# Regrouping the gelu pass of a two-layer spectral-attention block on Trainium2: both mixes, both first transforms, both groups of transposes, then the next synthesis

## The chip, the core and the metric

One core of a Trainium2 chip runs the whole kernel in one launch. The metric is the device time of an execution in microseconds. The kernel before was timed in five runs; its median is 575.03 us (572.42 to 576.11). Its profile is of one execution of 575.71 us, whose instructions span 573.7 us.

## The reference

The input x is (2, 56, 128, 128) in float32: two images with 56 planes of 128 x 128. Two layers of the same form follow each other. In each, all operators work by the plane, with a spectral convolution that keeps 32 x 16 modes. Cut to what matters here:

```
def layer(x):
    xn = inorm(x)                                   # per plane
    k, q, v = fno(xn, K), fno(xn, Q), fno(xn, V)     # 8 heads
    out = softmax(q k^T / 128) v                    # over the 56 planes
    att = inorm(fno(out, P) + x)
    an = inorm(att)
    h = gelu(inorm(spectral(an, M0)) + skip(an))    # over 128 x 128
    h = inorm(spectral(h, M1)) + skip(h)
    return inorm(h) + att

x = x + layer(group_norm(x))    # twice, with two sets of weights
```

The gelu stage is the line of h with gelu: it needs a plane's values in space, applies gelu to them, and the next line needs the modes of the result.

## The kernel before, in words

All arithmetic is float32. Each of the two images (b = 0 and 1) has a working plane tile P[b] of 128 x 8192, and X2 holds the input of both. Work on modes is done by TensorE (PE) with small matrices. Spatial values are formed by two sets of matmuls that add up in PSUM: `synthesis` (matmul at L751) turns modes into space, and `mixed` (L766) adds the attention's mix of the 56 planes of X2.

A gelu pass handles one image in four steps A = 0 to 3, each with two halves v = 0 and 1 of 128 x 1024 values. For each A:

- `synthesis(A)`: 16 matmuls into two PSUM pairs, one for each half (32 records in the trace, because each float32 matmul appears as two).
- `mixed(A, v)`: 4 matmuls onto a pair; then ScalarE (ACT) applies gelu from the pair into P[b] (L819), and VectorE (DVE) takes statistics of it, two instructions per half (L821).
- `turn_back(A, v)`: 8 transposes on PE (L801) of the gelu's result into another pair, and a copy on ACT into one of the two buffers hT[v] (L802).
- `forward(A, v)`: 4 matmuls (L789) from hT[v], the first transform of the next convolution, into a bank shared by both halves; after the second half a DVE copy to FB[b] (L794).

A pair is two PSUM banks. The pool of pairs has three buffers, the pool of single banks has two[...]. A new pair therefore waits until the pair three allocations ago has been read.

The order of the work is written out by hand in generators. Each `yield` gives a planned cost; `_woven` takes a leading chain (small dependent steps) and runs units of the bulk generators between its steps until the cost that the chain asks for is used up. In each layer there are two gelu passes: gelu(0), woven with `norms_chain` of image 1 (sums at L441, scalar steps on DVE and a square root on ACT at L721, spread of rows at L436, DVE steps L729 to L743, inverse at L401 with stream transposes on DVE at L406); and gelu(1), woven with `h_chain` of image 0 (L835 to L876, modes at L386, product at L419, sums at L441, square roots at L859 and L866, spread at L436, a scale at L878 copied at L880, inverse at L401). The inverse of each chain makes the modes from which the next pass's synthesis starts. After the second pass follows `end`, in which synthesis and mix are done once more, DVE (L916) and GpSimd (L918) add the terms, and the DMA queue of SyncE moves the result out (L896).

A scheduler puts the instructions on each engine's queue, largely in the order in which they are issued, but it lets an instruction pass others where its own inputs are ready earlier.[...]

Of the kernel before, what the change touches and what calls it, by code (L numbers as in the profile page):

```python
# [166 lines left out]
def fno_layers(ctx: ExitStack, tc: tile.TileContext, x, out, weights, small, const):  # L167
# [13 lines left out]
    def bank():  # L181
        return ps.tile([N, 512], F32, name="bank")

    def pair():
        return pq.tile([N, 2, 512], F32, name="pair")
# [267 lines left out]
    def new_stats(b):  # L453
        return little(f"stats{b}", [N, 16, 6])
# [292 lines left out]
    def synthesis(A, both, Z):  # L747
        for e in range(4):
            for j in range(4):
                o = 64 * (8 * A + 2 * e)  # L750
                T.matmul(  # L751
                    both[j // 2][:, j % 2, N * e : N * e + N], lhsT=Z[32 * j : 32 * j + 32, o : o + N],
                    rhs=C["gw"][32 * j : 32 * j + 32, :], start=(e == 0), stop=False, tile_position=(32 * j, 0),
                    skip_group_check=True,
                )

    def mixed(L, b, A, v, p, Bs):

        for c in range(2):
            s = 16 * A + (8 * v + 4 * c if L == 0 else 8 * c + 4 * v)
            for r in range(2):
                q = slice(64 * r, 64 * r + K + 1)
                T.matmul(  # L766
                    p[64 * c : 64 * c + 64, r, :], lhsT=Bs[q, :], rhs=X2[q, b, s : s + 4, :].rearrange("p e w -> p (e w)"),
                    start=False, stop=True, tile_position=(64 * r, 64 * c), skip_group_check=True,
                )

    def gelu(L, b, st):
        stats = st["stats"] = new_stats(b)
        banks = {}

        def at(A, v):
            return P[b][:, 2048 * A + 1024 * v : 2048 * A + 1024 * v + 1024]

        def forward(A, v):
            if v == 0:
                banks[A] = bank()  # L780
            f1, t = banks[A], hT[v]
            for q in range(4):
                if L == 0:
                    dst = f1[32 * q : 32 * q + 32, 224 * v : 224 * v + 224].rearrange("p (r m) -> p r m", r=2)
                    src = t[:, :, q].rearrange("p r c k -> p r (c k)")
                else:
                    dst = f1[32 * q : 32 * q + 32, :448].rearrange("p (c j k) -> p c j k", c=2, j=4)[:, :, 2 * v : 2 * v + 2]
                    src = t[:, :, q].rearrange("p r c k -> p c r k")
                T.matmul(  # L789
                    dst, lhsT=C["fw"], rhs=src, start=(v == 0), stop=True, tile_position=(0, 32 * q),  # L790
                    skip_group_check=True,
                )
            if v == 1:
                V.tensor_copy(FB[b][:, 448 * A : 448 * A + 448], f1[:, :448])  # L794

        def turn_back(A, v):
            h3, p = at(A, v), pair()
            for r in range(2):
                for e in range(4):
                    o = 512 * r + N * e  # L800
                    T.transpose(p[:, r, N * e : N * e + 120], h3[:120, o : o + N], ident[:120, :120])  # L801
            S.copy(  # L802
                hT[v].rearrange("p r e c k -> p (r e) c k"),
                p.rearrange("p r (e c k) -> p (r e) c k", e=4, c=2)[:, :, :, :K],
            )

        for A in range(6):
            if A < 4:
                both = [pair(), pair()]
                synthesis(A, both, st["Z"])  # L810
                yield 1.0
            if A > 1:
                forward(A - 2, 1)
                yield 0.4
            for v in range(2):
                if A < 4:
                    mixed(L, b, A, v, both[v], st["Bs"])
                    h3 = at(A, v)
                    S.activation(h3, both[v].rearrange("p r m -> p (r m)"), AF.Gelu)  # L819
                    for r in range(2):  # L820
                        V.bn_stats(stats[:, 4 * A + 2 * v + r, :], h3[:, 512 * r : 512 * r + 512])  # L821
                    yield 0.9
                if 0 < A < 5:
                    turn_back(A - 1, v)
                    yield 0.8
            if 0 < A < 5:
                forward(A - 1, 0)
                yield 0.4

    def h_chain(L, b, st):  # L830
        (par, d), fb, D = prs[L], FB[b], st["D"]
# [102 lines left out]
    st = [[{}, {}], [{}, {}]]  # L934
# [8 lines left out]
    for L in range(2):  # L943
        s0, s1 = st[L]
        more = relay(cpt, tcs, stage[:, :1024], [(16, 16), (32, 4)]) if L == 0 else ()
        _run(_woven(chain(modes_chain(L, 1, stats[1], s1), more), gram(0, s0)))
        build(WTv, tcs, 16, range(0, 8, 2))
        build_m(tcs)
        _run(_woven(gram_chain(L, 0, s0), _with(gram(1, s1), scale_x(0, s0))))
        _run(_woven(gram_chain(L, 1, s1), scores(L, 0, s0)))  # L950
        _run(_woven(softmax_chain(L, 0, s0), values(L, 0, s0)))
        _run(_woven(mix_chain(L, 0, s0), heads(L, 0, s0)))
        _run(_woven(
            norms_chain(L, 0, s0), _with(scores(L, 1, s1), scale_x(1, s1)),
            _woven(softmax_chain(L, 1, s1), values(L, 1, s1)), _woven(mix_chain(L, 1, s1), heads(L, 1, s1)),
        ))
        if L == 0:
            nc.sync.dma_start(out=stage[:, :1088], in_=weights[1].rearrange("p m r n t -> p (m r n t)"))
            par, d, cpt, tcs = prepare(1, G, G)
            prs[1] = par, d  # L960
        _run(_woven(norms_chain(L, 1, s1), gelu(L, 0, s0)))
        _run(_woven(h_chain(L, 0, s0), gelu(L, 1, s1)))
        stats = [new_stats(b) for b in range(B)] if L == 0 else [None, None]
        more = relay(cpt, tcs, stage[:, :1024], [(0, 16), (16, 16), (32, 4)]) if L == 0 else ()
        _run(_woven(chain(h_chain(L, 1, s1), more), end(L, 0, s0, stats[0])))
        if L == 0:
            o = _PARTS["fx"][0]
            nc.sync.dma_start(out=Ct[:, o:], in_=const["all"][:, N_CONST:])
            build(WUv, tcs, 0, range(0, 8, 2))
            _run(_woven(modes_chain(1, 0, stats[0], st[1][0]), end(0, 1, s1, stats[1])))  # L970
        else:
            _run(end(1, 1, s1, None))
# [52 lines left out]
```

## Time and profile before

| What | Value |
|---|---|
| median of five runs | 575.03 us |
| lowest and highest | 572.42, 576.11 us |
| the profiled execution, its own time | 575.71 us |
| its span, first to last instruction | 573.7 us |
| mean granted clock of TensorE | 0.88 of full speed |
| busy share of PE, DVE, ACT, POOL | 82%, 58%, 33%, 32% |
| gelu(0), layer 0 (first synthesis to the next pass's) | 173.0 to 206.1 us |
| gelu(1), layer 0 | 206.1 to 243.0 us |
| gelu(0), layer 1 | 440.4 to 471.4 us |
| gelu(1), layer 1 | 471.4 to 508.2 us |

A busy PE is a time in which matmul records lie open. It says nothing on the clock at which they run; that is a column of its own, PEclk, in tenths or as a share of full speed. In a timeline, a line is a run of like instructions: start, duration, engine, line of the code, operation, output and inputs, shapes, number of records, and in brackets the idle time ahead of it with what ended it. PEld are the weight loads of PE, which run beside the matmuls.

### The profile page before, as it was taken

How to read it: one execution, taken by the hardware profiler on the slowest of the kernel's cores; microseconds unless marked ns; L12 is line 12 of the kernel's file. 1: busy time of each engine (PE TensorE's matmuls, PEld its weight loads, DVE VectorE, ACT ScalarE, POOL GpSimd, SP SyncE). 2: the span in 40 equal slices, each digit the busy share in tenths (PEclk: the TensorE clock that was granted, in tenths of full speed). 3: DMA queues.
4: the chain of work that ended last, by engine and by line, in shares of the span. 5: the costliest groups of instructions: out<-in, count | busy, mean ns of one | idle time of the engine just before them, and what ended most of it. 6: DMA issues, size and time to landing. Idle time of an engine off the chain costs nothing.

```text
span 573.7 us, 15727 instructions
## 1 busy us (share of the span) xinstructions
PE 468.7 (82%) x7110; PEld 322.3 (56%) x7110; DVE 333.9 (58%) x577; ACT 191.2 (33%) x238; POOL 181.3 (32%) x190
## 2 busy tenths in 40 slices
PE   2446989889989999888587949987999999979480
PEld 1422949649866555545473447755957555645240
DVE  0576478811335774778649995831161767584661
ACT  2334131150536456413203314114343755712000
POOL 2450516800083000054375761620000000016566
PEclk9999689785997998998768969978799999898596
DMA  8992000050000000036334631040000000006687
GB/s 207 207 205 31 4 1 3 3 141 3 3 3 2 2 1 1 1 81 210 113 98 127 193 110 27 3 103 2 2 2 3 1 2 1 2 18 192 193 247 283
DMA packets 16307, 40.64 MB, mean 71 GB/s; under 512 B 2528, under 2 KB 3296, under 8 KB 16224
## 3 DMA queue, kind: packets, MB, share of 16 engines
q1 hardware_dynamic: 15520, 38.25, 24.7%
q10 hardware_dynamic: 720, 1.39, 1.0%
q8 instruction: 56, 0.92, 0.7%
q14 instruction: 11, 0.09, 0.1%
HBM read 24.69 MB, written 14.68 MB: 69 GB/s over the span
## 4 chain that ended last, share of the span: by engine, by line
PE 46%; DVE 20%; DMA 11%; ACT 6%; issue 6%; POOL 6%; SPq 3%; POOLq 1%; ACTq 0%; DVEq 0%
PE pair L766 6%; PE pair L801 5%; PE pair L595 5%; DVE X L550 4%; PE pair L689 4%; PE pair L751 4%; PE bank L511 3%; PE bank L576 3%; DVE stats L373 3%; POOL X L918 3%; SPq L896 3%; PE bank L789 3%; DMA xr<-x 3%; POOL P L918 2%; DMA X<-store 2%
## 5 line engine op out<-in xcount | busy, mean ns | idle before, releaser
L821 DVE BATCH_NORM_STATS2 stats<-P 128x6 f32<-128x512 f32 x64 | 40.5, 680 | 21.5 <-ACT P L819 21.4
L916 DVE SCALAR_TENSOR_TENSOR P<-P,hs,pair 128x1024 f32<-128x1024 f32 x32 | 40.1, 1269 | 18.1 <-PE pair L766 18.1
L550 DVE TENSOR_TENSOR X<-X,gvr 120x1024 f32<-120x1024 f32 x32 | 48.7, 1550 | 0.0
L918 POOL TENSOR_TENSOR X<-P,xr 128x1024 f32<-128x1024 f32 x16 | 39.1, 2450 | 29.5 <-DVE P L916 14.3
L373 DVE BATCH_NORM_STATS2 stats<-P 128x6 f32<-128x448 f32 x64 | 35.7, 612 | 19.8 <-ACT P L368 10.1
L819 ACT ACTIVATE P<-pair 128x1024 f32<-128x1024 f32 x32 | 32.6, 1026 | 33.6 <-PE pair L766 33.0
L801 PEld LDWEIGHTS pair<-C,P 120*128 120x128 f32 x256 | 28.3, 149 | 23.3 <-issue 12.3
L395 POOL MEMSET WT<- 128x256 f32 x4 | 1.3, 313 | 124.7 <-PE bank L789 89.9
L766 PE MATMUL pair<-X,Bs 57*64 57x512 f32 x256 | 40.1, 668 | 0.0
L511 PE MATMUL bank<-P 128*64 128x56 f32 (+1 forms) x1024 | 38.8, 244 | 0.0
L511 PEld LDWEIGHTS bank<-P 128*64 128x64 f32 (+1 forms) x1024 | 37.2, 158 | 2.9 <-issue 2.6
L766 PE MATMUL pair<-X,Be 57*64 57x512 f32 x256 | 38.1, 692 | 0.0
L595 PEld LDWEIGHTS pair<-xf,WU 64*64 64x64 f32 x1024 | 34.6, 142 | 5.1 <-issue 4.2
L595 PE MATMUL pair<-xf,WU 64*64 64x56 f32 x1024 | 37.3, 227 | 0.0
L801 PE MATMUL pair<-C,P 120*128 120x120 f32 x256 | 36.3, 287 | 0.4 <-ACT P L819 0.2
L751 PE MATMUL pair<-C,WT 32*128 32x128 f32 x512 | 26.3, 312 | 12.4 <-DVE P L916 7.4
L751 PEld LDWEIGHTS pair<-C,WT 32*128 32x128 f32 x512 | 21.2, 207 | 24.5 <-DVE P L916 10.6
L802 ACT COPY WT<-pair 128x896 f32<-128x896 f32 x32 | 28.8, 906 | 13.6 <-PE pair L801 13.3
L363 PE MATMUL pair<-C,X 56*128 56x56 f32 x256 | 17.4, 292 | 18.9 <-DMA X<-x 12.9
L341 POOL TENSOR_TENSOR WT<-tc,C 128x1024 f32<-128x1024 f32 x8 | 26.5, 3341 | 20.0 <-ACT tc L335 11.9
L371 ACT COPY P<-pair 128x896 f32<-128x896 f32 x16 | 14.4, 902 | 47.1 <-PE pair L365 47.1
L363 PEld LDWEIGHTS pair<-C,X 56*128 56x128 f32 x256 | 14.9, 198 | 24.4 <-DMA X<-x 12.3
(249 smaller groups left out, 884.2 us busy)
## 6 DMA issues: line engine op xcount, KB each, us to landing
X<-x SPq DMA_DIRECT2D x16, 448.0 KB
xr<-x SPq DMA_DIRECT2D x32, 224.0 KB
store<-X SPq DMA_DIRECT2D x32, 224.0 KB
out<-P SPq DMA_DIRECT2D x32, 224.0 KB
xr<-store SPq DMA_DIRECT2D x16, 224.0 KB
X<-store SPq DMA_DIRECT2D x16, 224.0 KB
C<-const_all ACTq DMA_DIRECT2D x1, 621.0 KB
stage<-weights ACTq DMA_DIRECT2D x1, 544.0 KB
```

The lines of the kernel that those rows point to most:

```text
L363: T.transpose(p[:, c, o : o + K], X2[q, b, i, :], ident[q, q], tile_position=(64 * c, 0))
L373: V.bn_stats(stats[:, 2 * g + s, :], dst[:, 448 * s : 448 * s + 448])
L511: T.matmul(p[u : u + m, :K], lhsT=P[b][:, K * i : K * i + m], rhs=plane[b][:, i, :], start=(i < 2), stop=(i == N - 1), tile_position=(0, u ...
L550: V.tensor_tensor(v, v, _bc(st["gvr"][:120], 1, 8), ALU.mult)
L595: T.matmul(p[64 * e : 64 * e + 64, k, K * a : K * a + K], lhsT=WUv[64 * e : 64 * e + 64, t + k, a, :], rhs=xv[64 * e : 64 * e + 64, t + k, ...
L751: T.matmul(both[j // 2][:, j % 2, N * e : N * e + N], lhsT=Z[32 * j : 32 * j + 32, o : o + N], rhs=C["gw"][32 * j : 32 * j + 32, :], start ...
L766: T.matmul(p[64 * c : 64 * c + 64, r, :], lhsT=Bs[q, :], rhs=X2[q, b, s : s + 4, :].rearrange("p e w -> p (e w)"), start=False, stop=True, ...
L801: T.transpose(p[:, r, N * e : N * e + 120], h3[:120, o : o + N], ident[:120, :120])
L819: S.activation(h3, both[v].rearrange("p r m -> p (r m)"), AF.Gelu)
L821: V.bn_stats(stats[:, 4 * A + 2 * v + r, :], h3[:, 512 * r : 512 * r + 512])
L916: V.scalar_tensor_tensor(h3, h3, st["hs"], both[v].rearrange("p r m -> p (r m)"), ALU.mult, ALU.add)
L918: G.tensor_tensor(dst, h3, back(n), ALU.add)
```

## The change

The four kinds of work of a pass are kept, and their number too. In the kernel before, the halves of different steps alternate: one mix, one group of transposes, the second mix, the second group of transposes, and the two first transforms at the end of this round and after the next synthesis. In the changed kernel a round does both mixes of A, then both first transforms of A-2, then both groups of transposes of A-1, then the synthesis of A+1. The first synthesis stands ahead of the loop. The planned costs are joined accordingly (1.8 for two mixes, 0.9 for two first transforms, 1.7 for two groups of transposes, 1.0 for a synthesis).

```diff
+        both = [pair(), pair()]
+        synthesis(0, both, st["Z"])
+        yield 1.0
         for A in range(6):
             if A < 4:
-                both = [pair(), pair()]
-                synthesis(A, both, st["Z"])
-                yield 1.0
-            if A > 1:
-                forward(A - 2, 1)
-                yield 0.4
-            for v in range(2):
-                if A < 4:
+                for v in range(2):
                     mixed(L, b, A, v, both[v], st["Bs"])
                     h3 = at(A, v)
                     S.activation(h3, both[v].rearrange("p r m -> p (r m)"), AF.Gelu)
                     for r in range(2):
                         V.bn_stats(stats[:, 4 * A + 2 * v + r, :], h3[:, 512 * r : 512 * r + 512])
-                    yield 0.9
-                if 0 < A < 5:
+                yield 1.8
+            if A > 1:
+                for v in range(2):
+                    forward(A - 2, v)
+                yield 0.9
+            if 0 < A < 5:
+                for v in range(2):
                     turn_back(A - 1, v)
-                    yield 0.8
-            if 0 < A < 5:
-                forward(A - 1, 0)
-                yield 0.4
+                yield 1.7
+            if A < 3:
+                both = [pair(), pair()]
+                synthesis(A + 1, both, st["Z"])
+                yield 1.0
```

## The prediction

> **What bounds the kernel now.** Read in this order: the page's busy shares, the chain of work that ended last, the timelines of the engines through the gelu passes, the granted clock in short windows.
>
> ```profile
> PE 468.7 (82%) x7110; PEld 322.3 (56%) x7110; DVE 333.9 (58%) x577; ACT 191.2 (33%) x238; POOL 181.3 (32%) x190
> ```
>
> TensorE leads, and in the chain the stretches 173 to 243 us (layer 0) and 440 to 508 us (layer 1) are nearly all PE groups: gelu(0) woven with norms_chain(1), then gelu(1) woven with h_chain(0). So only two things count: moments in which PE waits there, and its clock. Layer 1, timeline of PE (start, duration, records):
>
> ```profile
> 445.00 0.98 PE L441 MATMUL bank<-C,P 128*56 128x1 f32 x16
> 445.91 1.39 PE L751 MATMUL pair<-C,P 32*128 32x128 f32 x32
> 447.53 0.99 PE L441 MATMUL bank<-C,P 128*56 128x1 f32 x16 [0.23 <-ACT P L705]
> 448.45 1.09 PE L766 MATMUL pair<-X,Bs 57*64 57x512 f32 x8
> 449.47 1.04 PE L801 MATMUL pair<-C,P 120*128 120x120 f32 x8
> ...
> 494.46 1.72 PE L751 MATMUL pair<-C,P 32*128 32x128 f32 x32
> ...
> 503.85 1.78 PE L401 MATMUL pair<-WU,C 64*128 64x224 f32 x16 [0.48 <-DVE WU L876]
> ...
> 508.22 0.50 PE L751 MATMUL pair<-C,WT 32*128 32x128 f32 x6 [1.10 <-DVE WT L406]
> ```
>
> PE hardly waits. By piece of the chain, at full clock: S, a synthesis, 1.10 us; M, one mix, 1.02; T, eight transposes, 0.97; F, one first transform, 0.52. One A costs 1.10 + 2 x (1.02 + 0.97 + 0.52) = 6.12, and this does not change. Below, M(1), T(1) and F(1) mean both halves of A = 1, with the time at which they end. The 1.72 at 494.46 is an S that waits for ACT, which is switching tables:
>
> ```profile
> 488.74 1.28 ACT L859 ACT_TABLE_LOAD   x1
> ...
> 490.50 0.91 ACT L802 COPY WT<-pair 128x896 f32<-128x896 f32 x1 [0.20 <-PE pair L801]
> ...
> 492.28 1.28 ACT L819 ACT_TABLE_LOAD   x1
> 493.57 1.02 ACT L819 ACTIVATE P<-pair 128x1024 f32<-128x1024 f32 x1
> 494.50 0.90 ACT L802 COPY WT<-pair 128x896 f32<-128x896 f32 x1
> ```
>
> And the clock (layer 0; the last but two column is PEclk):
>
> ```profile
> 180.20:181.90 1.70, 1.70 (x14) 0.75 (x13) 0.88 (x7) 1.02 (x3) 0.00 (x0) 0.50 0.00 0
> ...
> 183.60:185.30 1.70, 1.70 (x12) 0.77 (x11) 1.29 (x2) 1.16 (x2) 0.00 (x0) 0.50 0.00 0
> ...
> 224.40:226.10 1.70, 1.70 (x12) 1.40 (x14) 1.63 (x9) 0.77 (x3) 0.00 (x0) 0.50 0.00 0
> 226.10:227.80 1.70, 1.70 (x9) 0.09 (x3) 1.27 (x8) 1.68 (x3) 0.00 (x0) 0.50 0.00 0
> ```
>
> Half clock for 6.8 us in layer 0's first pass, for 3.4 us in each second pass, and not at all in layer 1's first pass. Layer 0's first pass (S at 173.00 to the next S at 206.13) takes 33.1 us, layer 1's (440.42 to 471.38) 31.0: 2.15 us for two half-clock windows.
>
> **What the Trainium skill says.** "TensorE: Matmul & The Clock Gate", Part 1: PE runs at half clock unless it was busy in a free-running window of 3413 ns. The trace agrees: half-clock stretches begin near 224.24 and 490.45, 266.2 us or 78 such windows apart, and last one or two of them. Windows that turned it down held about 1.8 us of one-column sums (L441) and idle time; one with 1.5 us of idle time (248.1 to 251.5, PE idle until 249.62) did not. Records show 0.50 and 1.00 only, as the page has it. I estimate the limit as 1.6 us. "PSUM — Partial Sum Buffer", Engine vs sequencer instructions: ScalarE and VectorE are strict first-in-first-out, and matmuls complete in program order. The trace shows no overtaking. So the order in which the built program puts instructions on each engine is enough to work the queues through.
>
> **The change, worked through at layer 1's times and full clock.** No instruction, byte or DMA is added; SP and POOL keep their order. What moves: PE, ACT and DVE orders inside the two passes, and where the woven chain's steps fall, since a unit of the pass now ends every 0.9 to 1.8 instead of 0.4 to 1.0 of planned cost.
>
> *First pass.* S(1) now stands ahead of the chain's first sums. It needs the PSUM pair of the second gelu: first gelu 444.64 (unchanged), second ends 446.58. M(0) and the multiply end at 445.2, so PE waits 1.4; S(1) ends 447.5, the sums 448.6, M(1) 450.65, second sums 451.55, T(0) 453.5. Before, 0.9 us of sums covered this wait. ACT has both gelus (to 451.6), sqrt table 1.28, the square root, two copies of 0.91 (to 454.95), gelu table (to 456.2). S(2) needs the first copy (454.05): ends 454.75. M(2) 456.8, spread 457.25, F(0) 458.3, T(1) 460.25, S(3) 461.4. Now the chain's inverse (L401). Its input comes from DVE, which before did L729 to L734 in 2.35 us ahead of the next statistics; now four statistics (2.45) and an L794 (0.54) stand in between: 457.35 + 5.2 = 462.6. PE waits 1.2, with M(3) behind it. The inverse's second half needs the pair that its first half's stream transpose frees (463.55 + 1.65): 465.25 against 464.0, another 1.25. Then M(3) 467.7, F(1) 468.75, T(2) 470.7, F(2) and T(3) 473.65, F(3) 475.15; the next M starts at 476.05 against 474.32. **+1.75 us.**
>
> *Second pass.* From 476.05: S(1) waits for its gelus as before (479.45), M(1) 481.5, T(0) 483.45, L386 485.1, S(2) 486.2, multiply 487.25, M(2) 489.3, sums 491.1, F(0) 492.15, T(1) 494.1. Both gelus of A=2 lie ahead of the sqrt table, the copies behind it end at 495.05; S(3) needs only the first and runs 494.1 to 495.2, where before it ended 496.12. M(3) 497.25 (the gelu table is back at 496.7), F(1) and spread 498.75, T(2) 500.7. F(2) needs the bank of L880, whose ACT copy stands behind two T copies: 501.8, a wait of 1.0; F(2) 502.85. The inverse needs DVE's L878 behind L794: 503.65, a wait of 0.8; before 503.85. From there DVE's two stream transposes lead as before: next S at 508.0 against 508.22, with the last F and its DVE copy 0.1 nearer to before than that. **-1.85 us**: the table switches no longer hold PE, and the half clock that lay hidden behind them before costs nothing in this sum.
>
> So -0.1 per layer, -0.2 in all. After S the chain runs through DVE, POOL and the DMA queue, which are unchanged, so a shift passes on one for one.
>
> *Clock.* First sums: a window catches 1.6 us of idle time and sums in 1.8 of 3.41 phases (before 1.7 of 3.41): the same chance of one half, 2.15 us when it happens; 2.15 expected over two layers, which is what the profiled run paid. New: waits of 1.2 and 1.25 in 3.9 us catch a window in 1.25 of 3.41 phases, 0.37; a half-clock window does half its work, so it costs up to 3.41/2 = 1.7: 2 x 0.37 x 1.7 = 1.3. The 1.8 us of sums in the second pass: 0.59; before, the loss lay under ACT's wait (S(3) ended when ACT was done), now F, T, S and M follow with ACT ahead of them, so it is exposed: 2 x 0.59 x 1.7 = 2.0. Waits at F(2) and L401: 2 x 0.3 x 0.5 = 0.3. Sum +3.6, bounds 0 and 10 (all windows hit); below nothing -2.15 (layer 0 escapes).
>
> Total against the profiled execution (575.71; span 573.7 and 2.0 around it): 575.71 - 0.2 + 3.6 = 579.1. That run lies 0.7 above the median of 575.03, so on the median's scale **578.4 us**.
>
> **Rivals.** (1) *Neutral*: the passes exchange 1.75 for 1.85, and the clock costs no more than 0.5 beyond before's: 575.03 - 0.2 + 0.5 = 575.3. For it: PE's work is equal and both waits end in the same DVE chain. Against: the new waits and sums are as long as those that cost clock before. (2) *Faster*, the other side: by grouping, ACT's table switches fall between pairs of gelus and M and T never share a wait with them. The place is S(3) of each second pass; the price 1.65 - 1.10 there and what stands behind, up to 1.85 per layer. It decides if the first-pass inverse does not wait (DVE reaches L734 by 461.4 instead of 462.6 and a pair is free): then 2 x 1.75 of the first pass goes, and with only the last clock term: 575.0 - 0.2 - 3.5 + 0.3 = 571.6. For it: before, L401 never waited in the first pass. Against: the four statistics stand ahead in DVE's queue. (3) *Much slower*: first-pass loss is not handed back, since the second pass already waits for the same DVE chain: 575.0 + 2 x 1.75 + 3.6 = 582.1.
>
> **How the numbers follow.** The case of 578.4 has 0.44, rival 1 0.26, rival 2 0.16, rival 3 0.14. Within 0.5% (572.15 to 577.9) is about what a measurement of this kernel can tell from no change. The forecast case spreads by one clock window, 576.5 to 581, and leaves a fifth of itself (0.09) under 577.9: faster 0.16, same 0.26 + 0.09 = 0.35, slower 0.35 + 0.14 = 0.49. Range 572.5 to 582.5: it takes in all but the tails of rivals 2 and 3.
>
> **What would show it.** In the first pass: PE idle about 1.4 us ahead of S(1), L401 waiting over 1 us for DVE twice, the pass about 1.75 longer than layer 1's 31.0 at full clock. In the second pass: S(3) at 1.1 instead of 1.65, L401 not later against the pass's start than 27.6 us (503.65 - 476.05; before 29.5). PEclk 0.50 after the sums in the second pass with T and M at twice their length. Wrong if the waits at L401 are missing, or if the ends of the passes move while the kernel's end does not.

## The result, and the profile after

| | before | changed |
|---|---|---|
| median | 574.28 us (80 runs) | 577.26 us (43 runs) |
| lowest to highest | 570.10 to 580.19 | 570.34 to 589.88 |
| profiled execution, its span | 575.71, 573.7 | 577.89, 575.9 |
| mean granted clock of TensorE in it | 0.880 | 0.872 |

The ratio of changed to before is 1.0024, 95% interval 1.0008 to 1.0040. It leaves out the runs more than 1.5% above the fastest of their kernel, 15 of the changed kernel's 44 and 2 of before's 80, which the medians of the table take in. By the ratio the change costs 1.4 us, by the medians 2.98. In a later comparison (e7) the ratio was 1.0045 (1.0019 to 1.0070), 2.6 us, and the medians were 3.5 us apart. The change makes the kernel a little slower: less than the forecast's 0.6% by the ratios, about it by the medians.

Busy times hardly moved. In the changed code the gelu stands at L815, its statistics at L817, h_chain's steps two lines earlier than before.

```profile
PE 471.1 (82%) x7110; PEld 331.4 (58%) x7110; DVE 334.8 (58%) x577; ACT 188.9 (33%) x238; POOL 181.6 (32%) x190
```

Timeline of PE in the changed kernel, first pass of layer 1, against the lines 445.00 to 449.47 of before (start, duration, records, in brackets the idle time ahead):

```profile
441.56 1.95 PE L766 MATMUL pair<-X,Bs 57*64 57x512 f32 x16
443.33 1.10 PE L419 MATMUL pair<-P,WM 64*64 64x56 f32 x32
445.13 0.71 PE L751 MATMUL pair<-C,P 32*128 32x128 f32 x6 [0.70 <-ACT P L815]
446.04 1.16 PE L751 MATMUL pair<-C,P 32*128 32x128 f32 x26 [0.21 <-ACT P L815]
...
452.82 2.03 PE L751 MATMUL pair<-C,P 32*128 32x128 f32 x32
...
459.82 1.46 PE L751 MATMUL pair<-C,P 32*128 32x128 f32 x32
462.54 1.03 PE L401 MATMUL pair<-P,C 64*128 64x224 f32 x8 [1.26 <-DVE P L734]
463.50 1.07 PE L766 MATMUL pair<-X,Bs 57*64 57x512 f32 x4
465.35 1.03 PE L401 MATMUL pair<-P,C 64*128 64x224 f32 x8 [0.77 <-DVE P L406]
466.30 1.93 PE L766 MATMUL pair<-X,Bs 57*64 57x512 f32 x12
```

S(1) waits for a gelu (445.13), the inverse waits for DVE (462.54), its second half for a pair (465.35). Between them stand two things that carry no wait in brackets and yet are long: S(2) takes 2.03 (1.96 to the next start) instead of 1.10, and M(3) is cut into 4 and 12 records of 1.07 and 1.93. Before, S(2) had its 1.10 to the next start at 454.83, and the inverse ran in one piece without a wait:

```profile
453.73 1.17 PE L751 MATMUL pair<-C,P 32*128 32x128 f32 x32
...
458.34 1.78 PE L401 MATMUL pair<-P,C 64*128 64x224 f32 x16
```

DVE ahead of the inverse in the same kernel:

```profile
457.25 0.62 DVE L729 TENSOR_TENSOR P<-D,bank 128x448 f32<-128x448 f32 x1 [2.97 <-PE bank L436]
457.78 2.47 DVE L817 BATCH_NORM_STATS2 stats<-P 128x6 f32<-128x512 f32 x4
460.17 0.60 DVE L730 TENSOR_TENSOR P<-P,bank 128x448 f32<-128x448 f32 x1
...
462.16 0.24 DVE L734 TENSOR_SCALAR P<-dc,der 1x56 f32<-1x56 f32 x1
```

The four statistics of both halves stand in the middle of the chain's steps, as forecast. The second pass of layer 1, against 494.46 to 508.22 of before:

```profile
489.70 1.79 PE L441 MATMUL bank<-C,WU 128*56 128x1 f32 x32
...
494.11 1.41 PE L751 MATMUL pair<-C,P 32*128 32x128 f32 x32
...
500.73 0.38 PE L880 MATMUL bank<-r,C 56*128 56x1 f32 x2 [0.25 <-DVE WU L794]
501.59 0.96 PE L789 MATMUL bank<-WT,C 128*32 128x224 f32 x16 [0.48 <-ACT hs L882]
503.41 2.92 PE L401 MATMUL pair<-WU,C 64*128 64x224 f32 x16 [0.85 <-DVE WU L878]
506.26 2.35 PE L801 MATMUL pair<-C,P 120*128 120x120 f32 x16
508.54 0.48 PE L751 MATMUL pair<-C,WT 32*128 32x128 f32 x2
```

S(3) no longer stands behind the table switch (1.34 to its end, before 1.66). The inverse starts 26.44 us after the pass's first mix; before, 29.53. It runs at half clock here, and not after the sums. Short windows of the changed kernel (the last but two column is PEclk; two pairs, each a window and the one after it, cut where the clock changed and 3.41 us ahead of that):

```profile
230.83:234.24 3.41, 1.96 (x24) 1.33 (x26) 2.66 (x9) 0.92 (x3) 0.00 (x0) 1.00 0.00 0
234.25:237.65 3.40, 3.40 (x21) 2.75 (x18) 2.69 (x2) 0.00 (x0) 0.00 (x0) 0.50 0.00 0
500.49:503.89 3.40, 1.82 (x22) 1.19 (x24) 2.79 (x9) 1.05 (x3) 0.00 (x0) 1.00 0.00 0
503.91:507.31 3.40, 3.40 (x19) 2.75 (x16) 2.43 (x2) 0.00 (x0) 0.00 (x0) 0.50 0.02 5
```

PE was busy for 1.96 and 1.82 us of the windows ahead of the half-clock ones.

Lengths of the passes from first mix to the next pass's first mix, the clean measure of all that follows:

| us | first pass, layer 0 / 1 | second pass, layer 0 / 1 |
|---|---|---|
| before | 34.98 (two half-clock windows) / 32.17 | 35.93 / 35.93 (a half-clock window each) |
| changed | 35.42 / 35.41 | 34.52 / 34.52 (a half-clock window each) |

At full clock the first pass lost 3.24 us. Within the one pair of profiles the four passes differ by only +0.86, because before's layer 0 paid two windows and the changed kernel none; the rest of the 2.2 us between the spans lies outside the passes.

### The profile page after: what moved, and what is told of

The parts are those of the page before. It is cut to its first block, busy times and chain, and to the rows that moved or that the text cites. A ratio compares the mean times of both kernels' runs of the same rounds, so it can differ in the third digit from the quotient of the medians.

```text
span 575.9 us, 15723 instructions
## 1 busy us (share of the span) xinstructions
PE 471.1 (82%) x7110; PEld 331.4 (58%) x7110; DVE 334.8 (58%) x577; ACT 188.9 (33%) x238; POOL 181.6 (32%) x190
## 4 chain that ended last, share of the span: by engine, by line
PE 54%; DVE 23%; DMA 7%; ACT 6%; issue 5%; POOL 4%; SPq 1%; POOLq 0%; ACTq 0%; DVEq 0%
PE pair L766 7%; PE pair L751 5%; DVE X L550 4%; PE pair L595 4%; PE pair L801 4%; PE pair L689 4%; PE bank L511 3%; DVE stats L373 3%; PE bank L576 3%; PE bank L483 3%; DMA X<-store 3%; PE bank L441 2%; PE bank L789 2%; PE pair L401 2%; DVE P L918 2%
## 5 line engine op out<-in xcount | busy, mean ns | idle before, releaser
L817 DVE BATCH_NORM_STATS2 stats<-P 128x6 f32<-128x512 f32 x64 | 39.8, 678 | 14.6 <-ACT P L815 14.5
L766 PE MATMUL pair<-X,Be 57*64 57x512 f32 x256 | 41.1, 740 | 0.0
L511 PEld LDWEIGHTS bank<-P 128*64 128x64 f32 (+1 forms) x1024 | 38.9, 164 | 2.9 <-issue 2.4
L511 PE MATMUL bank<-P 128*64 128x56 f32 (+1 forms) x1024 | 40.5, 250 | 0.0
L815 ACT ACTIVATE P<-pair 128x1024 f32<-128x1024 f32 x32 | 31.0, 1020 | 27.2 <-PE pair L766 27.2
L595 PEld LDWEIGHTS pair<-xf,WU 64*64 64x64 f32 x1024 | 33.1, 137 | 4.8 <-issue 3.9
L595 PE MATMUL pair<-xf,WU 64*64 64x56 f32 x1024 | 35.8, 222 | 0.0
L751 PE MATMUL pair<-C,WT 32*128 32x128 f32 x512 | 27.9, 318 | 8.4 <-DVE P L918 5.8
L766 PE MATMUL pair<-X,Bs 57*64 57x512 f32 x256 | 33.4, 602 | 0.0
L801 PE MATMUL pair<-C,P 120*128 120x120 f32 x256 | 31.3, 276 | 0.0
L365 PEld LDWEIGHTS pair<-C,X 120*128 120x128 f32 x128 | 17.2, 172 | 20.5 <-POOL X L920 15.1
```

The source lines that it names most:

```text
L511: T.matmul(p[u : u + m, :K], lhsT=P[b][:, K * i : K * i + m], rhs=plane[b][:, i, :], start=(i < 2), stop=(i == N - 1), tile_position=(0, u ...
L595: T.matmul(p[64 * e : 64 * e + 64, k, K * a : K * a + K], lhsT=WUv[64 * e : 64 * e + 64, t + k, a, :], rhs=xv[64 * e : 64 * e + 64, t + k, ...
L751: T.matmul(both[j // 2][:, j % 2, N * e : N * e + N], lhsT=Z[32 * j : 32 * j + 32, o : o + N], rhs=C["gw"][32 * j : 32 * j + 32, :], start ...
L766: T.matmul(p[64 * c : 64 * c + 64, r, :], lhsT=Bs[q, :], rhs=X2[q, b, s : s + 4, :].rearrange("p e w -> p (e w)"), start=False, stop=True, ...
```

## The experiments

**Theories.** Theory Q, of queues and waits (later called work): the first pass loses to waits and to PE working below its packing, the second wins back less, and the sum of both at full clock is the result. Its rival, the clock: the passes nearly cancel, as the forecast's -0.2 says, and the loss is half-clock time, its +3.6. A line with numbers of L816, L818, L845 or L902 and above is the same code shifted by an added branch.

**e1 and e2: each pass alone.**

```diff
+        if b == 0:          # e1; e2 has b == 1
+            (the new order)
+        else:
+            (the old order)
```

> Only gelu(0), the pass woven with norms_chain, is regrouped; gelu(1) keeps the order of before, in both layers. Theory Q (queues): the first pass, first mix to the next pass's first mix, takes about 35.4 us in both layers (32.2 in the kernel before at full clock), because S(1) waits for a gelu, the inverse L401 waits for DVE and for a pair, and a synthesis or mix that is cut by a wait runs at half its packing; the second pass stays near 35.9. The kernel is 3 to 5 us slower than before. Theory C (clock): the queues come out even and only half-clock windows differ; both passes within 1 us of before, the kernel within 1.5 us of before.

> Only gelu(1), the pass woven with h_chain, is regrouped; gelu(0) keeps the order of before. Theory Q: the second pass falls from 35.9 to 34.5 us, or to 33.3 if no half-clock window meets its inverse, the first pass stays as before; the kernel is 2.5 to 5 us faster than before, and faster than both kernels. Theory C: within 1.5 us of before.

| | median, us | ratio to before (95%) | first passes | second passes |
|---|---|---|---|---|
| e1 | 580.54 (6 runs) | 1.0156 (1.0119 to 1.0193) | 35.42, 35.43 | 35.92 (window), 35.58 |
| e2 | 569.33 (22 runs) | 0.9929 (0.9903 to 0.9954) | 32.18, 32.17 | 34.51 (window), 33.79 |
| before, same chip | 573.68 (43 runs) | | | |

At full clock the lengths repeat to 0.02 us in both layers and all kernels, so each pass is a fixed sum of work and waits to which half-clock windows are added. First pass: 32.17 to 35.42, **+3.25**. Second pass at full clock: 35.58 to 33.79, **-1.79**. Per layer +1.46, in all +2.9 us; counted from the 35.93 that before's profile shows, with its half-clock windows, +2.2. The whole kernel lost 1.4 and 2.6 us by the two ratios and 2.98 and 3.5 by the medians, so the passes give the size of the loss as far as the runs can tell. e1 lost more than expected, 6.9 us in the medians and 9 by the ratio, where 2 x 3.25 = 6.5 is what its passes give.

What the second pass wins shows at S(3). In the order of before at full clock (e1, layer 1) ACT does a table load of 1.28 us ahead of h_chain's first square root (at 495.02) and another ahead of the next gelu (at 498.56), and it is this gelu (over at 500.88) that frees the pair for the second half of S(3). S(3) starts at 499.17, and its second half waits:

```profile
500.93 1.16 PE L751 MATMUL pair<-C,P 32*128 32x128 f32 x16 [0.60 <-ACT P L845]
```

S(3) takes 2.85 us to the next start at 502.02, against 1.34 in the new order. The 1.66 of before's own profile is shorter because half clock had already delayed PE ahead of it.

**e3: the chain's spread earlier.** The fourth planned cost of norms_chain for image 1:

```diff
-        yield 3.5
+        yield 2.0 if b else 3.5
```

> The changed kernel with the spread of rows (L436) of norms_chain for image 1 issued ahead of the mixes of A = 2, so that DVE does L729 to L734 before four statistics instead of behind them; nothing else moves by hand. Theory Q: both waits at L401 (1.26 and 0.77 us) and the cut of the third mixes go; S(3) may wait for the stream transposes in their place; first pass 33.5 to 34.2 instead of 35.4, the kernel 2.5 to 4 us faster than the changed one. Theory C: the waits are covered elsewhere, under 1 us.

It was slower: 581.41 us (6 runs), ratio 1.0155 (1.0113 to 1.0198). PE in its first pass, layer 1:

```profile
466.47 1.04 PE L801 MATMUL pair<-C,P 120*128 120x120 f32 x8 [2.31 <-DVE P L406]
467.44 2.66 PE L751 MATMUL pair<-C,P 32*128 32x128 f32 x32
470.03 3.69 PE L766 MATMUL pair<-X,Bs 57*64 57x512 f32 x16
```

and two windows there:

```profile
464.10:467.50 3.40, 1.09 (x11) 0.88 (x10) 3.40 (x4) 0.91 (x1) 0.00 (x0) 1.00 0.00 0
467.52:470.92 3.40, 3.40 (x36) 2.46 (x40) 0.45 (x1) 0.91 (x1) 0.00 (x0) 0.50 0.00 0
```

The inverse no longer waits for DVE. But its two halves hold two of the three pairs until DVE's stream transposes (L406) have read them, and the second half of T(1) needs one: one wait of 2.31 (2.32 in layer 0). In both layers half clock follows this wait, in layer 1 for two windows, after one with PE busy for 1.09 of 3.40. The first pass took 37.85 us in layer 1 and 35.89 in layer 0. It was not seen at full clock; my estimate, taking off what T(1), S(3), M(3) and F(1) took at half clock beyond their lengths at full clock in the changed kernel and before, is 34.3 in both layers, some 1.1 below the changed kernel and just outside theory Q's range. So the early spread did shorten the queue, by less than expected because I had followed the inverse's input and not its pairs, and half clock took back more than that. Of e1 to e4 it is also the one with a clearly lower mean clock, 0.872 over its six runs against 0.883 in before's 43.

**e4: the whole chain earlier.** The first planned cost of norms_chain for image 1:

```diff
-        yield 1.6
+        yield 0.5 if b else 1.6
```

> The changed kernel with the whole norms_chain of image 1 one step earlier: the multiply ahead of the first mixes and the first sums ahead of S(1), the spread between the transposes of A = 0. Theory Q: beside what the early spread gives, 0.9 us of sums cover the wait ahead of S(1); first pass 32.5 to 33.3, the kernel 4 to 5.5 us faster than the changed one, about 1 to 2 us faster than before. Theory C: no more than 1 us against the changed kernel, unless half-clock windows vanish from the first pass, which its profile would show in PEclk.

575.16 us (22 runs), ratio 1.0032 (1.0008 to 1.0057): 2.1 below the changed kernel's median, where 4 to 5.5 were expected, and by the ratio (1.0024 and 1.0045 for the changed kernel) no gain at all is shown. The chain's multiply now runs ahead of the first mix; counted from the end of the pass's first synthesis, the first pass of layer 1 takes 33.25 instead of 35.41; the second takes 33.81. The waits for a gelu and for DVE shrink, and stream transposes again hold pairs: 1.06 ahead of the second half of T(1), 0.50 ahead of S(3). By these lengths the kernel should stand 1 to 2 us below before, and its median stands 1.5 above. Its mean clock was lower, 0.879 against 0.883, which is worth about 1.5 us (see e7); the rest of the gap stays open.

**e5: the price of packing.** The kernel before, each synthesis issued pair by pair:

```diff
-        for e in range(4):
-            for j in range(4):
+        for e, j in [(e, 2 * h + k) for h in range(2) for e in range(4) for k in range(2)]:
+            if True:
```

> The kernel before, with each synthesis issued as all eight matmuls of the first pair and then all eight of the second (two row groups at a time instead of four). Same matmuls, same results. Theory packing: what the changed order lost in S(2), M(3) and the next S beyond its waits is that matmuls of different row groups run side by side only while both pairs are at hand; a step takes 0.11 us whether two or four row groups take part. Then a synthesis takes 2.0 instead of 1.10 us, and with 32 of them, a few hidden behind waits, the kernel gets 20 to 29 us slower: 594 to 603. Theory contention: a synthesis is set by the number of its matmuls and weight loads (32 records), and S(2) was long for another reason (ACT and DVE reading PSUM beside it): 1.1 to 1.3 us each, the kernel less than 5 us slower.

589.54 us (2 runs), ratio 1.0272 (1.0198 to 1.0347), +15.6: below the range that packing gave, far above contention's. A synthesis that waits for nothing:

```profile
452.65 1.72 PE L751 MATMUL pair<-C,P 32*128 32x128 f32 x32
```

It holds PE for 1.66 us (to the next start at 454.31) instead of 1.10. Not 2.0, since the second pair's matmuls join in before the first pair's are done. The 15.6 us are not all packing: in the profiled run 5.4 us of the difference lie ahead of the first synthesis (178.43 against 173.00), where nothing was changed, and the mean clock of the two runs was 0.868 against 0.883. The clean measure is the first pass at full clock: 33.63 and 33.62 against 32.17, so 1.46 for four syntheses; the rest of 4 x 0.56 = 2.24 can only lie behind waits, which was not looked at one by one. So the order of the same 32 records is worth half a synthesis, and this is what S(2) of the changed kernel pays. Two windows of 0.88 and 0.86 us from the start of a synthesis, S(2) of the changed kernel and S(3) of before:

```profile
452.82 1.04 PE L751 MATMUL pair<-C,P 32*128 32x128 f32 x13
```

```profile
462.81 1.06 PE L751 MATMUL pair<-C,P 32*128 32x128 f32 x28
```

13 records against 28. In S(2) two records start together, in before's S(3) four, and in both the next ones start 0.11 us later. So a step is no longer than before, only half filled, and theory contention falls. "TensorEngine Tiling (Array Packing)", Key Properties, says that tiles can execute in parallel; the trace adds that a group left out is not caught up. The code alternates the pairs, so it must be the scheduler that put these 13 records, about seven matmuls, of the first pair ahead of the second pair's (the trace does not name the pair of a record). The second pair waits for the first copy of T(0), which is over at 453.60; from 453.69 on more records join in.

**e6: the inverse after M(3).** The fifth planned cost of norms_chain for image 1:

```diff
-        yield 2.6
+        yield 5.0 if b else 2.6
```

> The changed kernel, with the chain's inverse of the first pass (L401) asked for 2.4 of planned cost later, so that it stands behind both halves of M(3) on TensorE. Theory waits (the first pass loses its 3.2 us in four places: S(1) 1.1, S(2) 0.9, the inverse's wait and S(3) 1.6, the split M(3) 1.9, less what grouping saves): the wait of 1.26 for DVE, the wait of 0.77 for a pair and the two halves of M(3) at half packing go, T(2) may wait up to 0.5 for a stream transpose; first pass 32.4 to 33.2 us instead of 35.4, the second unchanged at 33.8 to 34.5; the kernel 4 to 6 us faster than the changed one and 0 to 3 us faster than the kernel before. Theory chain (the DVE chain to the inverse sets the end of the pass, so moving the inverse back only moves the wait behind it): first pass 35 to 36, the kernel as the changed one or slower.

574.85 us (22 runs), 2.6 below the changed kernel on the same chip (577.42, e7), short of the 4 to 6 expected; ratio to before 1.0004 (0.9979 to 1.0029), by the ratios 2.4 below the changed kernel. First pass, layer 0, at full clock:

```profile
191.12 1.95 PE L766 MATMUL pair<-X,Bs 57*64 57x512 f32 x16
193.00 1.78 PE L401 MATMUL pair<-P,C 64*128 64x224 f32 x16
194.71 0.96 PE L789 MATMUL bank<-WT,C 128*32 128x224 f32 x16
195.60 1.04 PE L801 MATMUL pair<-C,P 120*128 120x120 f32 x8
197.49 1.04 PE L801 MATMUL pair<-C,P 120*128 120x120 f32 x8 [0.85 <-DVE P L406]
199.03 0.32 PE L801 MATMUL pair<-C,P 120*128 120x120 f32 x1 [0.50 <-DVE P L406]
```

33.64 us (36.50 in layer 1, with two half-clock windows): both waits at L401 and the split of M(3) are gone, 1.35 of waits for pairs come instead of the 0.5 expected. The net gain of 1.78 per pass is more than half of the lost 3.24; 2 x 1.78 = 3.6 is what the passes give, 2.6 what the medians show. The theory that DVE's chain to the inverse sets the pass's end falls.

**e7: the changed kernel again.** No edit.

> The changed kernel once more, beside the others on one chip, for a second sample of the clock. Theory work: passes of 35.4 and 33.8 us at full clock as before, so 2 x (3.25 - 1.78) = 2.9 us more than the kernel before at equal clock, and a mean clock within 0.004 of it; the median 1.5 to 4.5 us above. Theory clock (the forecast's 3.6 us): the mean granted clock lies 0.01 lower than in the kernel before, with half-clock stretches after the sums of the second pass.

577.42 us (22 runs), before 573.90 (43 runs). Passes 35.42, 35.41 and 33.79, 33.80, all at full clock: +1.1 to +1.5 per layer against 32.17 + 35.58 to 35.93. The mean granted clock of its runs is 0.885, that of before's 0.883; in the 44 runs of the first comparison it was 0.886. Across those 44 runs the time falls by 3.6 us for each 0.01 of clock, so the forecast's 3.6 us would have lowered the clock by 0.01. It did not fall.

**e8, e9, e10: the better version.** Only the second pass regrouped (e2, and again as e10), and in e8 and e9 the spread of h_chain earlier too:

```diff
         dg = rows_of(b, [(f_, par["gmo"][:K]), (c4[:, 2:3], r3[:, 1:2])])
-        yield 6.0
+        yield 4.4 if b == 0 else 6.0
```

> Only the second pass regrouped, and in it the spread of rows (L436) asked for 1.6 of planned cost earlier, so that it stands ahead of the first transforms of A=1 on TensorE and the first step of the inverse's input ahead of the four statistics of A=3 on DVE. Theory DVE (the second pass's end is set by DVE's queue ahead of the inverse, four statistics and the copies of the first transforms): the inverse starts 1 to 1.5 us earlier, the wait of 0.85 ahead of it and the 0.73 ahead of the first transforms go; second pass 32.3 to 33.2 instead of 33.8; the kernel 1 to 3 us faster than with the second pass regrouped alone (569.3), so 566.5 to 568.5. Theory PE (the matmuls set the second pass's end): 33.6 to 34, no gain.

> The version with only the second pass regrouped and its spread of rows earlier, once more, since its first result rests on six runs whose profiled one had a clock of 0.902. Theory work: passes of 32.17 and 33.28 us against 32.17 and 35.6 to 35.9 before, so 4.6 to 5.3 us less at equal clock: 568 to 570 where the kernel before stands at 573.9. Theory clock: part of the 8.6 us seen first is a property of the kernel (shorter idle stretches, fewer half-clock windows): mean clock 0.005 or more above the kernel with the plain second pass, and 564 to 566.5 again.

> Only the second pass regrouped, once more, on the same chip as the version with the earlier spread. Theory work: 33.79 instead of 35.6 to 35.9 in each second pass, 3.6 to 4.3 us less than before, and 0.5 per layer, 1.0 in all, more than with the earlier spread: 569.5 to 571. Theory clock: 3 us or more above the version with the earlier spread.

| | median, us | ratio to before (95%) | second pass at full clock |
|---|---|---|---|
| e8 | 565.30 (6 runs) | 0.9865 (0.9810 to 0.9920) | 33.28 |
| e9, the same kernel | 568.76 (14 runs) | 0.9927 (0.9900 to 0.9955) | 33.28 |
| e10, e2's kernel | 570.82 (22 runs) | 0.9959 (0.9933 to 0.9984) | 33.80, 33.78 |

Before stood at 573.90 us (43 runs) beside e8 and at 573.20 (35 runs) beside e9 and e10. e8's 8.6 us did not repeat: its six runs had a mean clock of 0.888 (0.902 in its profile), e9's fourteen 0.884, and e9 shows 4.4, which is what 2 x (35.58 to 35.93 - 33.28) = 4.6 to 5.3 gives. The gain per pass was 0.5 instead of 0.6 to 1.5, since a new wait appears, F(2) behind the DVE copy that frees its bank:

```profile
490.06 0.92 PE L789 MATMUL bank<-WT,C 128*32 128x224 f32 x10 [1.28 <-DVE WU L794]
```

Both versions beat the kernel before, by 0.4% and 0.7% with intervals that stay below 1, where those of the changed kernel stay above it.

## Why the forecast was wrong in size, point by point

The forecast's total, 578.4, is near the medians by luck, since its make-up is wrong: -0.2 of work and +3.6 of clock, where the runs show +2.2 to +2.9 of work and no loss of clock. Two errors of about the same size cancelled.

**First pass, +1.75 forecast, +3.24 measured: the step that failed.** Times from the first mix, layer 1:

| | forecast | measured |
|---|---|---|
| S(1) ends | 5.35 | 5.57 |
| T(0) ends | 11.35 | 11.26 |
| S(2) ends | 12.60 | 13.22 |
| S(3) ends | 19.25 | 19.72 |
| inverse starts, second half starts | 20.45, 23.10 | 20.98, 23.79 |
| M(3) ends | 25.55 | 26.61 |
| F(1) ends | 26.60 | 27.50 |
| next first mix | 33.90 | 35.41 |

All three waits were there and in place (S(1)'s 0.91 in two parts against 1.4, with S(1) still 0.22 late; the inverse's 1.26 against 1.2; its second half held by the stream transpose as said, 2.81 behind the first half against 2.65). The step "S(2) needs the first copy (454.05): ends 454.75" counted the matmuls left over as if they still ran four at a time; they took 1.09 after the copy's release instead of 0.7. M(3), cut by the inverse, the same: the 4 records ahead of the cut took 1.07, which the wait hid, but the 12 behind it took 1.87 to the next start, as much as 16 uncut (1.88), where the sum leaves them about 1.5. And the stretch from F(1) to the next mix was summed at 7.3; it takes 7.91, and before took 7.86 for the same work (465.44 to 474.32 without the one mix of 1.02 in it), since the next S is dealt out there in pieces between first transforms. That was in the trace of before. I had priced a synthesis as a block of 1.10 wherever it lay. S(2) is 0.7, M(3) 0.4 and this tail 0.6 of the missing 1.5, with 0.2 back elsewhere; e5 shows that packing has such a price, e6 what the inverse's waits and the cut M(3) cost together. The share of each alone was read from the timeline and not tried by itself.

**Second pass, -1.85 forecast.** The forecast started from before's profile, with its half-clock window: 35.93 to 33.79 is -2.14; from full clock to full clock it is -1.79. Right, and for the reasons given: S(3) free of the table switch (2.85 at full clock in the old order, 1.34 now; forecast 1.1), F(2) waiting 0.73 in two parts (forecast 1.0), the inverse 0.85 (0.8). It starts at 26.44, earlier than the bound of 27.6.

**Clock, +3.6 forecast, about 0 measured.** The price of a window was nearly right (1.7): where one followed the sums of a regrouped second pass (layer 1 of e3 and e9) the pass took 35.17 and 34.65 instead of 33.80 and 33.28, 1.37 more. The 2.15 for two windows in before's first pass was too low: from first mix to first mix the two layers differ by 2.81, because layer 1's first synthesis took 1.73 to layer 0's 1.10. The chance was wrong. In the eighteen regrouped second passes of nine profiled runs the sums lay wholly inside one window seven times, and the clock fell after two of these; I had given each pass 0.59. In the old order it had fallen each of the three times (both passes of before, layer 0 of e1). A half-clock window at the inverse came in four of the eighteen (both of the changed kernel's first profile, layer 0 of e2 and of e3) and cost 0.7. What a window must hold to turn the clock down stays open; my 1.6 us of idle time and sums came from too few windows. And "2.15 expected" for the old first pass was a sample of one execution.

**The rivals.** None took place as written. The first, at +0.3 us, lies below both intervals of the ratio (+0.5 to +2.3, and +1.1 to +4.0 in e7). The third, at 582.1, has its condition in e1, with the loss not handed back: 580.5, but from nearly twice the loss and no clock. The second is what e2 shows in its gain, and its condition (no wait of the inverse) is what e6 restores, where the time comes back to before's and not below, because S(1), S(2) and the pairs still cost 1.47 per pass against the 1.79 that the second pass wins.

## What to carry to other kernels

Price a packed group of matmuls by its steps, not its count: once a wait separates the partners, the part that goes ahead takes steps of full length that are only half filled, and no bracket in the timeline marks the loss. When work is regrouped, follow the buffers as well as the data: with three pairs, grouping both transposes and both mixes made S(2) wait for a copy and let the inverse hold pairs until DVE had read them. Try each place of a change by itself: here one of the two places was worth keeping, and the sum of both hid it.

## What was not expected of the hardware

- With PE busy by the records for all of a window, one-column sums inside it were followed by half clock in some passes (layer 1 of e9, below) and not in others (both layers of e4). At the inverse it fell after windows with PE busy for 1.82 and 1.96 us of 3.4. "TensorE: Matmul & The Clock Gate", Part 1, has it fall after an idle window; a part of one is enough here.

```profile
482.10:485.50 3.40, 3.40 (x58) 2.67 (x55) 2.44 (x9) 3.09 (x4) 0.00 (x0) 0.99 0.02 5
485.52:488.92 3.40, 3.40 (x27) 3.10 (x28) 1.57 (x6) 1.54 (x2) 0.00 (x0) 0.51 0.01 2
```

- The same kernel's mean granted clock varies between executions by 0.009 (one standard deviation over 44 runs), which is 3.3 us of its time and more than the change itself.
